# Two graph-attention layers on one core: layer 0's output projection by seven products, its flags and masks, and the order of the last step

## The chip, the cores and the metric

The kernel runs on one core of a Trainium2 chip. The metric is the device time of one execution in microseconds (us). The engines are named as in the profile: PE (matrix multiplication) with PEld (its weight loads), DVE (vector), ACT (scalar and activations), POOL (GpSimd), SP (the queue that issues DMAs).

## The reference

64 graphs of 256 nodes with 512 features each go through two layers. Both normalise, apply a ReLU, attend under an adjacency mask and add the result to their input:

```
# layer 0: 4 heads of 64, inner width 256
h = relu(layernorm(x));  q, k, v = h@Wq, h@Wk, h@Wv
a = softmax(where(adj, q k^T / 8, -max));  x = x + (a v) @ Wo + bo
# layer 1: 8 heads of 64, inner width 512
h = relu(layernorm(x));  q, k, v = split((layernorm(h)*gamma + beta) @ w_qkv^T)
a = softmax(where(adj | eye, q k^T / 8, -1e9));  x = x + (a v) @ w_out^T + b_out
```

In layer 0 a row of the mask without any neighbour gives equal weights; "flags" below (the tile `ne`) say which rows have a neighbour. All inputs but the mask are float32.

## The kernel before

**Steps and order.** A step handles two graphs, 512 tokens; there are 32 (NSTEP). Four tiles of 128 tokens (NT) make the rows `t` = 0 to 3; tiles 0 and 1 are the first graph. The order of instructions on PE, DVE, ACT and POOL is the order in which the program issues them. It comes from a list of events: `at(period, place, fn)` gives a function the key period × PERIOD + place, and at the end all events run in the order of their keys. Layer 0 of a step, layer 1 of the step before and the loads of the step after are so woven together; each engine then works its queue in order, and semaphores hold it where a tile is not ready. SP's DMAs keep the same order.

**Seven products.** The projections of queries and keys (`project_qk`, L755), layer 1's values (`project_v1`, L796) and layer 1's output projection (`combine1`, L821) are each made of seven half-size products instead of eight. `PRODUCT` (L398) names, for each product, the block of the weights and the block of the activations. Sums of blocks are made ahead: of weights once (`weight_sum`, L405), of activations in each step (`act_sums0`, L408, and `act_sums1`, L411 to L413) on POOL. `at_set` (L979) puts the seven one after another in the order `SET` or `SETC`; each has its matmuls at the front of its share and its evacuation from PSUM at the end of it. Products pass through four PSUM banks. `bank_of` (L729) lets product 2 go into the bank of product 1, 4 into that of 7 and 3 into that of 5 (`SHARED`), after the first of each pair has been read out; those banks are held meanwhile. `evacuate` (L684) writes a projection's blocks; `accumulate` (L703) adds a combination's products to the residual `xt` and keeps a common term `u`, which POOL adds to three blocks at L723 (in the last step DVE does).

**Layer 0's output projection** (`combine0`, L807) is plain: for each row tile t two matmuls of 128x128 by 128x512 and one addition to `xt` on DVE (L811). Its four tiles begin at place AT_C0 + 0.01, woven with the transposes of the next step's rows (`transpose_h`, L651, evacuated by ACT at L655 for layer 0 and L661 or L657 for layer 1). The attention outputs stand in `oT0`, one block for each pair of heads.

**Behind it** comes layer 1's normalisation: `norm1` takes the moments of a row of `xt` (L569 and L570 on DVE) and writes the centred ReLU on ACT (L623, L624); `norm1_rest` takes the moments of that, and POOL makes the factors (L639, L640, then `row_scales`, L579 to L581); `scale_row` (L585, ACT) scales the rows, which are then transposed. `norm0`, the same for layer 0, uses L569, L570 and L602.

**Attention of one pair of heads** is spread by `visit` (L986). At one place stand, for the pair before: weighing the values (L896) with ACT's copy to oT (L914), key sums (L930), and on DVE the reciprocals (L940) with their guard (L941), which SP spreads over partitions with eight DMAs (L955) and POOL multiplies in (`normalise`, L960). For the present pair: scores (L853), the masks' addition on DVE (L877), exponentials on ACT (L882) and sums of key halves on POOL (L887). In layer 0 POOL also multiplies two query blocks by the flags (L765).

**Masks.** `masks` (L550) makes both layers' additive masks from the turned adjacency `adT`: n1 first (L555, three buffers), n0 from n1 times the flags (L558), then n1 without its diagonal (L564).

**The ends.** In step 0 weights are still turned into place (`weight_block`, L463 on PE, L468 on DVE and ACT) between the sets. In the last step the order of layer 1 is first query/key set, layer 1's combination of the step before, second query/key set, values; the plain combination of layer 0 stands ahead of the first set.

Of the kernel before, what the change touches and what calls it, by code (L numbers as in the profile page):

```python
# [315 lines left out]
def fast_path(  # L316
# [80 lines left out]
    B_OF = ((0, 8, 7), (1, 3, 1))  # L397
    PRODUCT = {1: (0, 0), 2: (1, 1), 3: (6, 2), 4: (3, 6), 5: (2, 3), 6: (4, 4), 7: (5, 5)}  # L398
# [8 lines left out]
    def act_sums0(b, eng=nc.gpsimd):  # L407
        eng.tensor_tensor(b[:, 3], b[:, 7], b[:, 0], ALU.subtract)  # L408

    def act_sums1(b, eng=nc.gpsimd):  # L410
        eng.tensor_tensor(b[:, 4], b[:, 2], b[:, 3], ALU.subtract)  # L411
        eng.tensor_tensor(b[:, 5], b[:, 2], b[:, 7], ALU.subtract)
        eng.tensor_tensor(b[:, 6], b[:, 1], b[:, 4], ALU.subtract)  # L413
# [3 lines left out]
    HC, HP1 = NC // 2, PR1 // 2  # L417
    wqk0 = const.tile([P, NB, HC, 2, H0], FP, name="wqk0")
    wv0 = const.tile([P, NC, I0], FP, name="wv0")
    wo0 = const.tile([P, PR0, D], FP, name="wo0")  # L420
# [6 lines left out]
    def first_weights():  # L427
        for i in range(2):
            for k, w in enumerate((wq, wk)):
                nc.sync.dma_start(  # L430
                    wqk0[:, 2 * i:2 * i + 2, :, k, :].rearrange("p j c o -> p (j c) o"),
                    w[:, i * H0:(i + 1) * H0].rearrange("(c p) o -> p c o", p=P),
                )
        nc.sync.dma_start(wv0, wv.rearrange("(c p) o -> p c o", p=P))
        nc.sync.dma_start(wo0, wo.rearrange("(c p) o -> p c o", p=P))
        for v, t in ((bo, bo_b), (b_out, bout_b)):
            nc.sync.dma_start(t, bass.AP(tensor=v.tensor, offset=v.offset, ap=[[0, P], [1, D]]))
        gbr = sm.tile([2 * NC, P], FP, name="gbr", tag="inv", bufs=1)
        nc.scalar.dma_start(gbr[:NC], gamma.rearrange("(c p) -> c p", p=P))
        nc.scalar.dma_start(gbr[NC:], beta.rearrange("(c p) -> c p", p=P))  # L440
        return gbr
# [108 lines left out]
    def masks(s):  # L550
        st = S[s]
        adT = st["adT"]
        n1 = st["n1"] = act.tile([P, NIC, G, N], BF, name="n1", bufs=3)
        n0 = st["n0"] = act.tile([P, NIC, G, N], BF, name="n0")
        nc.gpsimd.tensor_scalar(n1, adT, -1.0, BIG, op0=ALU.add, op1=ALU.mult)  # L555

        for kc in range(NIC):
            nc.gpsimd.tensor_tensor(  # L558
                n0[:, kc].rearrange("p g n -> p (g n)"),
                n1[:, kc].rearrange("p g n -> p (g n)"), st["ne"], ALU.mult,  # L560
            )
        for kc in range(NIC):
            v = n1[:, kc, :, kc * P:(kc + 1) * P]
            nc.gpsimd.tensor_tensor(v, v, offdiag, ALU.mult)  # L564
# [7 lines left out]
    def row_scales(s, var, rows=slice(0, NT)):  # L572

        st = S[s]
        if rows.start == 0:
            st["r"] = stat.tile([P, NT], FP, name="r", bufs=3)
            st["mr"] = stat.tile([P, NT], FP, name="mr", bufs=3)
# [37 lines left out]
    def norm1(s, t):  # L615
        st, x1 = S[s], S[s]["xt"]
        if t == 0:
            st["mv"] = stat.tile([P, NT, 3], FP, name="mv1", bufs=2)
            st["mean"] = stat.tile([P, NT, 2], FP, name="mg", bufs=2)
            st["h"] = act.tile([P, NT, D], FP, name="h")  # L620
# [9 lines left out]
    def norm1_rest(s, t):  # L630
        st = S[s]
# [4 lines left out]
        if t % part == part - 1:  # L636
            rows = slice(t + 1 - part, t + 1)
# [3 lines left out]
            row_scales(s, ve, rows)  # L641
# [101 lines left out]
    def project_qk(s, lyr, a, n):  # L743
# [3 lines left out]
        if n == 1:  # L747
            for pr in (a, a + half):
                st["qk", lyr, pr] = sm.tile([P, 2, T], FP, name="qk", bufs=3)
# [53 lines left out]
    def combine0(s, t):  # L803
        st = S[s]
        bank = mm_tile([P, D])
        for pr in range(PR0):
            nc.tensor.matmul(  # L807
                bank, st["oT0"][:, pr, t // NIC, t % NIC * P:(t % NIC + 1) * P], wo0[:, pr, :],
                start=(pr == 0), stop=(pr == PR0 - 1),
            )  # L810
        return lambda: nc.vector.tensor_tensor(st["xt"][:, t, :], bank, st["xt"][:, t, :], ALU.add)  # L811

    def combine1(s, n):
        st = S[s]
        if n == 1:
            st["u"] = sm.tile([P, NIC, HD], FP, name="u", bufs=1)
        bank, first = bank_of(st, "c", n, HD)
        wa, ba = PRODUCT[n]
        for t in range(NIC):
            for c in range(HP1):  # L820
                nc.tensor.matmul(  # L821
                    bank[:, t, :], st["oT1"][:, ba, c, t * P:(t + 1) * P], wo1[:, wa, c, :],
                    start=first and (t, c) == (0, 0), stop=(t, c) == (NIC - 1, HP1 - 1),
                    skip_group_check=True,
                )
        return lambda: accumulate(n, bank, token_rows(st["xt"], HD), st["u"], s == NSTEP - 1)
# [17 lines left out]
    def scores(s, lyr, pr):  # L844
# [21 lines left out]
        if last and pr in (1, 2):  # L866
            pd = (wo0, wv0)[pr - 1].rearrange("p a b -> p (a b)").rearrange("p (e g n) -> p e g n", e=2, g=G)
# [21 lines left out]
    def weigh(s, lyr, pr, first):  # L889
# [11 lines left out]
        if lyr == 0:  # L901
            if first:
                st["oT0"] = act.tile([P, PR0, G, N], FP, name="oT0")
            dst = st["oT0"][:, pr]
        else:
            if first:
                st["oT1"] = act.tile([P, NB + 1, HP1, N], FP, name="oT1")
            b0, b1, step = B_OF[pr // HP1]
            dst = st["oT1"][:, b0:b1:step, pr % HP1, :]
# [56 lines left out]
    PERIOD = 6.13  # L966
# [17 lines left out]
    SETC = (1, 5, 2, 6, 7, 3, 4)  # L984

    def visit(period, w, prev, cur, later=0.0):  # L986

        w -= 0.0003
        if 0 <= prev[0] < NSTEP:
            at(period, w, weigh_out, *prev)  # L990
            at(period, w, key_sums, *prev[:3])
            at(period, w + later, invert, *prev[:3])
            at(period, w + (0.63 if prev[1:3] == (1, 1) else 0.55), normalise, *prev[:3])
        if 0 <= cur[0] < NSTEP:
            at(period, w, scores, *cur)
            at(period, w + later, mask_scores, *cur, 0)
            at(period, w + 0.05, exponentials, *cur, 0)
            at(period, w + 1 / 7, mask_scores, *cur, 1)
            at(period, w + 0.18, exponentials, *cur, 1)
            at(period, w + 0.2, key_halves, *cur, 0)  # L1000
            at(period, w + 0.3, key_halves, *cur, 1)

    AT_C0, AT_Q0, AT_V0, AT_H1, AT_C1 = 3.0, 3.57, 4.57, 5.13, 5.131
    LAST_QK = 4.0
    for s in range(-1, NSTEP - 1):
# [6 lines left out]
        visit(p, 3.685 if tail else AT_Q0 + 2 / 7, (s, 1, 1, False), (s, 1, 3), 0.03 if tail else 0.0)  # L1012
        if s >= 0:
            visit(p, LAST_QK + 3 / 7 if tail else AT_V0, (s, 1, 3, False), (s + 2, 0, 0))
# [3 lines left out]
    for w, i, pr in (  # L1018
        (LAST_QK + 1, 5 / 7, 0), (LAST_QK + 1 + 3 / 7, 5 / 7, 2), (LAST_QK + 3, 5 / 7, 1), (LAST_QK + 3 + 2 / 7, 4 / 7, 3)
    ):  # L1020
        visit(p, w, none, (NSTEP - 1, 1, pr))
        at(p, w + i - 0.0005, key_sums, NSTEP - 1, 1, pr)
        at(p, w + i, invert, NSTEP - 1, 1, pr)
# [8 lines left out]
    for s in range(NSTEP):  # L1032
# [14 lines left out]
        if s < 2:  # L1047
            at(p, (3.72, 2.72)[s], neighbours_rows, s)
            at(p, (3.855, 3.59)[s], neighbours_turn, s)
# [3 lines left out]
        at(p, (3.7125, 3.583)[s] if s < 2 else 2.2, adjacency_turn, s)  # L1053
        at(p, (3.87, 3.74)[s] if s < 2 else 2.75, masks, s)
        if s == 0:
            at(p, AT_C0, first_transposes)
        else:
            for c in range(NC):
                at(p, AT_C0 + 0.14 * (c // 2) + 0.001 * c if s > 1 else 2.9292 + 0.0001 * c, transpose_h, s, 0, c)
        at(p, AT_C0 + 0.1, lambda s=s: act_sums0(S[s]["hT"]))  # L1060
        at(p, AT_C0 + (0.2 if s != 1 else 0.101), lambda s=s: act_sums1(S[s]["hT"]))
# [7 lines left out]
        at(p, 1.0 if s else 0.0, load_x, s)  # L1069
        at(p, 1.8 if s else 1.55, first_bias, s)  # L1070
        back = 0.0 if s else 0.13
        for t in range(NT):
            at_dense(p, AT_C0 + 0.01 + 0.14 * t - back, 0.14, combine0, s, t)
            at(p, AT_C0 + 0.3 + 0.14 * t - back if (s, t) != (NSTEP - 1, 3) else 3.69, norm1, s, t)
            at(p, ((3.55, 3.7, 4.05, 4.2) if s < NSTEP - 1 else (3.55, 3.6, 3.7, 3.705))[t] - back, norm1_rest, s, t)
            at(p, 3.62 + 0.08 * t if 0 < s < NSTEP - 1 else 6.5 + 0.1 * t, second_bias, s, t)
            at(p, 4.5 + 0.1 * t if 0 < s < NSTEP - 1 else (4.25 if s == 0 else 3.71) + 0.003 * t, scale_row, s, t)

        for c in range(NC):
            at(p, (AT_H1 if s < NSTEP - 1 else 3.8) + 0.0001 * c, transpose_h, s, 1, c)  # L1080
        at(p, AT_C1 + 0.15 if s < NSTEP - 1 else 3.95, lambda s=s: act_sums0(S[s]["hT"], nc.gpsimd if s < NSTEP - 1 else nc.vector))
        at(p, AT_C1 + 0.5 if s < NSTEP - 1 else 3.96, lambda s=s: act_sums1(S[s]["hT"], nc.gpsimd if s < NSTEP - 1 else nc.vector))
        p = s
        if s < NSTEP - 1:
# [4 lines left out]
            at(p, 4.55 if not last else LAST_QK + 0.99, lambda s=s: act_sums0(S[s]["oT1"]))  # L1089
            at(p, AT_C1 + 0.1 if not last else LAST_QK + 1.0, lambda s=s: act_sums1(S[s]["oT1"]))  # L1090
            at_set(p, AT_C1 if not last else LAST_QK + 1, SETC, combine1, s)
            at(p, 6.3, store, s)
        else:
            p = s - 1
            at_set(p, LAST_QK, SET, project_qk, s, 1, 0)
            at_set(p, LAST_QK + 2, SET, project_qk, s, 1, 1)
# [3 lines left out]
            at_set(p, LAST_QK + 4.1, (1, 5, 2, 3, 6, 7, 4), combine1, s)  # L1100
# [5 lines left out]
    for i in range(4):  # L1106
        at(-2, 3.01, weight_sum, nc.vector, wqk0, i)
    at(-2, 4.0, lambda: blocks.extend(weight_loads()))
# [63 lines left out]
```

## Time and profile before

| | |
|---|---|
| median of 3 runs (lowest, highest) | 3401.17 us (3400.61, 3402.93) |
| the profiled execution's own time | 3401.54 us |
| its span, first to last instruction | 3399.3 us |
| PE, PEld busy | 3373.3 us (99%), 2621.7 us (77%) |
| DVE, ACT, POOL busy | 1919.5 (56%), 1243.2 (37%), 1991.2 (59%) |
| one step in the middle, by the starts of the same set | 104.69 us |
| first value set of layer 1 begins | 114.2 us |

Each float32 matmul (but for the transposes) stands in the profile as two instructions. A group's row has its line, engine, operation and tiles, the count, the busy time in us and mean ns of one, and then the idle time before them and what ended it. Matmuls overlap, so the mean of one is longer than the distance from start to start. A row of the order of time has start, length in us, engine, line and operation, count, and in brackets an idle time before and who ended it.

### The profile page before, as it was taken

The numbers are of one execution on the slowest core, as the hardware profiler recorded it, in microseconds if no ns is written. First come the engines' busy times: TensorE is split into PE (matmuls) and PEld (weight loads), VectorE is DVE, ScalarE is ACT, GpSimd is POOL, SyncE is SP. The second block draws the span as 40 slices with busy tenths as digits, with TensorE's granted clock in tenths as the row PEclk, the third lists the DMA queues.
The fourth block names the chain that finished last, engine by engine and source line by source line (L and its number), as shares of the span: only waits on it lengthen the run. The fifth ranks groups of instructions, "written<-read, shape, count | busy, mean of one in ns | idle before, by whom it ended". The sixth has DMA issues, their size and how long they took to land.

```text
span 3399.3 us, 59198 instructions
## 1 busy us (share of the span) xinstructions
PE 3373.3 (99%) x22602; PEld 2621.7 (77%) x22602; DVE 1919.5 (56%) x3402; ACT 1243.2 (37%) x2193; POOL 1991.2 (59%) x1858
## 2 busy tenths in 40 slices
PE   8999999999999999999999999999999999999999
PEld 6777777787777877778777777777787777877777
DVE  6755556555565555555555655556555555555565
ACT  4433443333333334433344333343333443334431
POOL 5655665556655556655576556665555655556632
PEclk9999999999999999999999999999999999999999
DMA  4111111211111211111111111111121111111111
GB/s 129 46 56 57 48 39 46 58 57 54 32 48 56 58 54 33 48 55 56 58 43 44 46 58 57 53 32 48 57 58 52 34 47 57 57 58 41 32 41 42
DMA packets 167697, 173.89 MB, mean 51 GB/s; under 512 B 59624, under 2 KB 112368, under 8 KB 167408
## 3 DMA queue, kind: packets, MB, share of 16 engines
q1 hardware_dynamic: 167008, 169.78, 16.9%
q8 instruction: 180, 2.95, 0.4%
q14 instruction: 109, 0.89, 0.1%
q10 hardware_dynamic: 400, 0.27, 0.0%
HBM read 85.99 MB, written 33.62 MB: 35 GB/s over the span
## 4 chain that ended last, share of the span: by engine, by line
PE 97%; DVE 1%; ACT 0%; issue 0%; DMA 0%; POOL 0%; SPq 0%; DVEq 0%; POOLq 0%
PE mm L755 34%; PE mm L796 12%; PE mm L821 11%; PE sc L853 11%; PE sc L896 10%; PE mm L782 6%; PE mm L807 6%; PE mm L651 3%; PE mm L930 2%; PE mm L543 0%; DVE bs L569 0%; ACT h L585 0%; DVE wqk L405 0%; DVE wqkv L405 0%; DVE inv L940 0%
## 5 line engine op out<-in xcount | busy, mean ns | idle before, releaser
L887 POOL TENSOR_TENSOR pd<-p 128x512 f32<-128x512 f32 x378 | 477.2, 1278 | 631.6 <-ACT p L882 523.3
L755 PE MATMUL mm<-hT,wqkv 128*128 128x256 f32 x3584 | 800.0, 382 | 2.6 <-DVE hT L411 1.4
L755 PEld LDWEIGHTS mm<-hT,wqkv 128*128 128x128 f32 x3584 | 673.8, 190 | 112.6 <-issue 23.1
L882 ACT ACTIVATE p<-p 128x512 f32<-128x512 f32 x768 | 459.1, 629 | 478.8 <-DVE p L877 477.9
L940 DVE RECIPROCAL inv<-mm 128x128 f32<-128x128 f32 x384 | 339.7, 926 | 367.6 <-PE mm L930 330.9
L877 DVE TENSOR_TENSOR p<-sc,n 128x512 f32<-128x512 f32 x768 | 481.2, 682 | 4.2 <-PE sc L853 4.2
L914 ACT COPY oT<-sc 128x512 f32<-128x512 f32 x188 | 110.2, 586 | 993.6 <-PE sc L896 993.6
L755 PE MATMUL mm<-hT,wqk 128*128 128x256 f32 x1792 | 403.4, 382 | 0.7 <-ACT wqkv L468 0.6
L796 PE MATMUL mm<-wqkv,hT 128*128 128x256 f32 x1792 | 396.1, 381 | 0.0
L821 PE MATMUL mm<-wo,oT 128*128 128x256 f32 x1792 | 393.3, 379 | 1.0 <-DVE xt L712 0.7
L960 POOL TENSOR_TENSOR oT<-oT,invb 128x512 f32<-128x512 f32 x188 | 240.9, 1282 | 261.0 <-DMA invb<-inv 253.3
L755 PEld LDWEIGHTS mm<-hT,wqk 128*128 128x128 f32 x1792 | 338.4, 191 | 69.5 <-DVE inv L940 9.9
L853 PE MATMUL sc<-qk 64*128 64x256 f32 x3072 | 384.1, 389 | 0.0
L796 PEld LDWEIGHTS mm<-wqkv,hT 128*128 128x128 f32 x1792 | 337.6, 190 | 56.3 <-issue 11.4
L821 PEld LDWEIGHTS mm<-wo,oT 128*128 128x128 f32 x1792 | 337.6, 190 | 47.7 <-issue 1.5
L896 PE MATMUL sc<-p,v 128*32 128x256 f32 x6144 | 370.7, 382 | 0.0
L853 PEld LDWEIGHTS sc<-qk 64*128 64x128 f32 x3072 | 281.2, 186 | 104.2 <-issue 77.6
L896 PEld LDWEIGHTS sc<-p,v 128*32 128x32 f32 x6144 | 180.3, 109 | 162.0 <-issue 61.5
L723 POOL TENSOR_TENSOR xt<-xt,u 128x512 f32<-128x512 f32 x93 | 118.1, 1270 | 245.6 <-DVE xt L716 183.9
L585 ACT ACTIVATE h<-h,mr,r 128x512 f32<-128x512 f32 x252 | 197.4, 809 | 115.4 <-POOL mr L581 115.3
L782 PE MATMUL mm<-wv,hT 128*128 128x256 f32 x1024 | 230.3, 382 | 0.0
L807 PE MATMUL mm<-wo,oT 128*128 128x512 f32 x512 | 230.3, 593 | 0.0
(123 smaller groups left out, 3675.1 us busy)
## 6 DMA issues: line engine op xcount, KB each, us to landing
invb<-inv SPq DMA_DIRECT2D x1528, 32.0 KB, 1.8
xt<-in_x_dram SPq DMA_DIRECT2D x32, 1024.0 KB, 9.8
h<-in_x_dram SPq DMA_DIRECT2D x31, 1024.0 KB, 6.2
out_dram<-xt SPq DMA_DIRECT2D x31, 1024.0 KB, 4.5
ne<-row SPq DMA_DIRECT2D x30, 256.0 KB, 4.4
ad<-in_adj_dram SPq DMA_DIRECT2D x32, 128.0 KB
wr<-in_L_gnn_w_qkv_dram SPq DMA_DIRECT2D x3, 1024.0 KB, 13.5
h<-in_x_dram SPq DMA_DIRECT2D x4, 256.0 KB, 2.7
```

The source lines that it names most:

```text
L755: nc.tensor.matmul(bank[:, k, :], w[:, wa, c, k, a * P:(a + 1) * P], st["hT"][:, ba, c, :], start=first and (k, c) == (0, 0), stop=(k, c) ...
L782: nc.tensor.matmul(bank, st["hT"][:, b0 + t // NIC * step, c % HC, i:i + P], wv0[:, c, :], start=(c == 0), stop=(c == NC - 1),)
L796: nc.tensor.matmul(bank[:, t, :], st["hT"][:, ba, c, t * P:(t + 1) * P], wqkv1[:, wa, c, 2, :], start=first and (t, c) == (0, 0), stop=(t, ...
L807: nc.tensor.matmul(bank, st["oT0"][:, pr, t // NIC, t % NIC * P:(t % NIC + 1) * P], wo0[:, pr, :], start=(pr == 0), stop=(pr == PR0 - 1),)
L821: nc.tensor.matmul(bank[:, t, :], st["oT1"][:, ba, c, t * P:(t + 1) * P], wo1[:, wa, c, :], start=first and (t, c) == (0, 0), stop=(t, c) ...
L853: nc.tensor.matmul(sc[g][e][:, kc, :], qk[rows, 1, k0:k0 + P], qk[rows, 0, g * N:(g + 1) * N], start=True, stop=True,)
L877: nc.vector.tensor_tensor(p[e][:, g], sc[e], neg[:, :, g, :], ALU.add)
L882: nc.scalar.activation(p[e][:, g], p[e][:, g], AF.Exp, scale=SCALE)
L887: eng.tensor_tensor(pd[:, e], p[e][:, :, 0, :], p[e][:, :, 1, :], ALU.add)
L896: nc.tensor.matmul(po[r0:r0 + 32, g, :], st[f"v{lyr}"][:, g * NIC + kc, pr * P + r0:pr * P + r0 + 32], p[r0 // DH][:, g, kc, :], start=(kc ...
L940: nc.vector.reciprocal(inv[:, i * P:(i + 1) * P], sums[:, i * P:(i + 1) * P])
L960: nc.gpsimd.tensor_tensor(dst, dst, invb, ALU.mult)
```

## The change

Layer 0's output projection becomes seven products, by a function that serves both layers. `wo0` and `oT0` get the seven blocks' layout, DVE sums wo0's blocks once and POOL those of oT0 in each step. Both outputs keep seven blocks (`O_OF`) where oT1 had eight. In step 0 and the last step DVE adds the common term, else POOL.

```
-    wo0 = const.tile([P, PR0, D], FP, name="wo0")
+    wo0 = const.tile([P, NB, HP0, HD], FP, name="wo0")
...
-    def combine0(s, t):
-        bank = mm_tile([P, D])
-        for pr in range(PR0):
-            nc.tensor.matmul(
-                bank, st["oT0"][:, pr, t // NIC, t % NIC * P:(t % NIC + 1) * P], wo0[:, pr, :],
-        return lambda: nc.vector.tensor_tensor(st["xt"][:, t, :], bank, st["xt"][:, t, :], ALU.add)
...
+    def combine(s, lyr, n):
         st = S[s]
         if n == 1:
             st["u"] = sm.tile([P, NIC, HD], FP, name="u", bufs=1)
+        oT, w, half = st[f"oT{lyr}"], (wo0, wo1)[lyr], (HP0, HP1)[lyr]
         bank, first = bank_of(st, "c", n, HD)
         wa, ba = PRODUCT[n]
         for t in range(NIC):
+            for c in range(half):
                 nc.tensor.matmul(
+                    bank[:, t, :], oT[:, ba, c, t * P:(t + 1) * P], w[:, wa, c, :],
...
+        at_once = s == NSTEP - 1 or (s, lyr) == (0, 0)
+        return lambda: accumulate(n, bank, token_rows(st["xt"], HD), st["u"], at_once)
...
+    SETC0 = (1, 6, 5, 2, 7, 3, 4)
...
+        at(p, 1.75 if s else 1.8, lambda s=s: act_sums0(S[s]["oT0"]))
+        at(p, 1.76 if s else 2.48, lambda s=s: act_sums1(S[s]["oT0"]))
+        edge = 0 if s == 0 else 1 if s == NSTEP - 1 else 2
+        for i, n in enumerate(SETC0 if s else SETC):
+            if edge == 1:
+                at_dense(p, 1.99905 + 0.00008 * i, 0.00107, combine, s, 0, n)
+            else:
+                at_dense(p, AT_C0 + (-0.12 if s == 0 else 0.14) + i / 14, 1 / 14, combine, s, 0, n)
...
+        at(-2, AT_V0, weight_sum, nc.vector, wo0, i)
```

The masks are made by two functions, each from adT; n1 has two buffers instead of three, the query/key tile two instead of three (the last step's first set uses a free part of wqk0), and in the middle steps n1 is made later, at place 5.7. The flags stay float32.

```
+    def mask0(s):
+        n0 = st["n0"] = act.tile([P, NIC, G, N], BF, name="n0")
+        nc.gpsimd.tensor_scalar(n0, st["adT"], -1.0, BIG, op0=ALU.add, op1=ALU.mult)
         for kc in range(NIC):
+            v = n0[:, kc].rearrange("p g n -> p (g n)")
+            nc.gpsimd.tensor_tensor(v, v, st["ne"], ALU.mult)
+    def mask1(s):
+        n1 = st["n1"] = act.tile([P, NIC, G, N], BF, name="n1", bufs=2)
+        nc.gpsimd.tensor_scalar(n1, st["adT"], -1.0, BIG, op0=ALU.add, op1=ALU.mult)
```

The order changes with it. PERIOD goes from 6.13 to 6.2. The transposes of layer 0 stand together ahead of the combination. The visit that stood after two products of layer 0's query/key set stands before the set, so in the middle of a step the order on PE is transposes, combination, visit, query/key set. The rows of layer 1's norm are taken in the order 2, 3, 0, 1 and later, inside that set:

```
-    AT_C0, AT_Q0, AT_V0, AT_H1, AT_C1 = 3.0, 3.57, 4.57, 5.13, 5.131
-    LAST_QK = 4.0
+    AT_C0, AT_Q0, AT_V0, AT_H1, AT_C1 = 3.0, 3.64, 4.64, 5.2, 5.201
+    LAST_QK = 3.0
...
+    NORM1 = (2, 3, 0, 1)
...
+            at(p, ((3.315, 3.32, 3.39, 3.41), (2.2, 2.25, 2.4, 2.45), (3.79, 3.8, 3.93, 3.94))[edge][k], norm1, s, k)
+                p, ((3.4, 3.42, 3.43, 3.435), (2.3, 2.35, 2.5, 2.55), (4.075, 4.22, 4.23, 4.36))[edge][k],
+                norm1_rest, s, k,
...
+            at(p, 6.5 + 0.1 * k if edge < 2 else AT_V0 + 0.01 * k, second_bias, s, k)
...
-            at_set(p, LAST_QK + 2, SET, project_qk, s, 1, 1)
+            at_set(p, LAST_QK + 1, SET, project_qk, s, 1, 1)
...
-            at_set(p, AT_C1 if not last else LAST_QK + 1, SETC, combine1, s)
+            at_set(p, AT_C1 if not last else LAST_QK + 2, SETC, combine, s, 1)
```

For the last step, layer 0's combination stands right behind layer 1's values of the step before; then come that step's second query/key set, the last step's transposes, its two query/key sets one behind the other, the combination of the step before, and the last values.

## The prediction

> **What bounds the kernel now.** I read the page first (engine shares, then the chain that ended last), then the groups, TensorE's waits, the order of time in one step of the steady middle, and last the two ends with the granted clock.
>
> ```profile
> span 3399.3 us, 59198 instructions
> PE 3373.3 (99%) x22602; PEld 2621.7 (77%) x22602; DVE 1919.5 (56%) x3402; ACT 1243.2 (37%) x2193; POOL 1991.2 (59%) x1858
> ...
> PE 97%; DVE 1%; ACT 0%; issue 0%; DMA 0%; POOL 0%; SPq 0%; DVEq 0%; POOLq 0%
> ```
>
> The chain runs through PE for 97% of the span. In the waits PE stands still from 100 to 3250 us for 0.8 us only; all else lies in the first 100 and the last 150 us. So a matmul left out of a middle step is time saved, if no new wait opens, and a wait of PE's costs its full length.
>
> ```profile
> L821 PE MATMUL mm<-wo,oT 128*128 128x256 f32 x1792 | 393.3, 379 | 1.0 <-DVE xt L712 0.7
> ...
> L807 PE MATMUL mm<-wo,oT 128*128 128x512 f32 x512 | 230.3, 593 | 0.0
> ```
>
> Each matmul of the program stands here as two instructions. L807 is layer 0's combination: 16 instructions a step. L821 is layer 1's, already by seven products: 56 a step. The change turns L807's 16 into 28 of L821's kind. What each takes, in order of time:
>
> ```profile
> 1927.39 1.09 PE L651 MATMUL mm<-ident,h 128*128 128x128 f32 x8
> 1928.32 1.88 PE L807 MATMUL mm<-wo,oT 128*128 128x512 f32 x4
> 1930.04 1.04 PE L651 MATMUL mm<-ident,h 128*128 128x128 f32 x8
> 1930.91 5.32 PE L807 MATMUL mm<-wo,oT 128*128 128x512 f32 x12
> 1936.06 3.62 PE L755 MATMUL mm<-hT,wqk 128*128 128x256 f32 x16
> ...
> 1965.64 12.25 PE L821 MATMUL mm<-wo,oT 128*128 128x256 f32 x56
> 1977.83 1.93 PE L896 MATMUL sc<-p,v 128*32 128x256 f32 x32
> ```
>
> From start to next start L807 takes 1.72 + 5.15 = 6.87 us a step (0.429 each). L821 takes 12.19 for 56, so 6.10 for 28; about 0.09 of the 12.19 is the step into the narrow matmuls of L896, which every such block shows and which exists before and after (without it 0.216 each, 6.05).
>
> **The sum, against the profiled execution's 3401.54 us** (span 3399.3 and 2.2 around it; the median of the three runs is 0.4 lower).
>
> *1. PE work.* Saved per step 6.87 − 6.10 = 0.77 to 6.87 − 6.05 = 0.82, say 0.80: 32 steps, **−25.6**. Nothing else on PE changes in number: the transposes, the block of L896/L930/L853 that moves from inside the first query/key set to before it, and the turns remain.
>
> *2. New waits in the 30 middle steps.* Layer 0's combination had plain sums; now products share banks, and its sums come 3 on POOL and 6 on DVE, with one copy on ACT. Four places are tight. T is the first transpose, S the first score matmul of the next block.
> - Product 4 goes into product 7's bank, and only product 3 (0.86) lies between. Needed: lag to DVE 0.20 (1967.57, where L708 starts, less 1965.64 and a product of 1.73), the add 0.69 (L712), release to PE about 0.15 (the row at 3391.23 starts 0.05 after DVE's end and its first load costs 0.1). 1.04 against 0.86: **0.18** lost. In layer 1 a product is 1.73 and hides this.
> - Product 2 goes into product 1's bank after ACT has copied it. ACT first has four L655 and two exponentials: 0.69 + 4 × 0.49 + 2 × 0.53 + 0.59 = T + 4.3, and PE is there at T + 1.74 + 3 × 0.86 = T + 4.3. I take 0.03; bounds 0 and 0.2.
> - In the query/key set product 4 waits for DVE's evacuation of 7. DVE's queue from S: 0.14, reciprocals and guard 2.15, four masks 2.45, two adds 1.22, and now seven moments pairs ahead, 5.67:
>
> ```profile
> 1935.22 0.69 DVE L569 BATCH_NORM_STATS2 bs<-xt 128x6 f32<-128x512 f32 x1
> 1935.94 0.18 DVE L570 BATCH_NORM_AGGREGATE mv<-bs 128x2 f32<-128x6 f32 x1
> 1936.04 0.66 DVE L569 BATCH_NORM_STATS2 bs<-h 128x6 f32<-128x512 f32 x1
> ...
> 1942.04 1.77 DVE L940 RECIPROCAL inv<-mm 128x128 f32<-128x128 f32 x2 [1.53 <-PE mm L930]
> ```
>
>   (A pair is 0.81 from start to start.) The evacuation starts at S + 11.6, and PE can go on at S + 12.5. PE is there at S + 1.93 + 6 × 1.754 = S + 12.45. **0.05** lost; bounds 0 and 0.4, as everything on DVE in 12 us stands in front of it.
> - POOL's row scales (1.79 from 1950.81 to 1952.60) and then the flag product L765 (1.29) end at about S + 16.25; the scores that need them come at S + 16.5, less 0.15. Hidden by 0.1; if not, up to 0.2.
>
> Together 0.26 a step, **+7.8**; bounds 0.1 and 0.9 a step (3 and 27 us). Each tenth that I miss a step is 3 us.
>
> *3. The head.* Four sums of the new wo0 (128x256, DVE) stand before the last moments of step 1, whose rows PE already awaits (L651). Half of a 128x512 sum: 0.34 (L408 on DVE, 0.68) to 0.85 (L405, up to 1.7 beside POOL); I take 0.45, **+1.8**. Step 0 makes 9 DVE operations instead of 4 (5 × 0.61 = 3.1) in a chain for which PE waits 1.1 us now at L651. ACT's copies of L786 now queue behind the copy of u and the rows of norm1, and hold banks of the next products and weight blocks. I lay out 1.7 at the combination's third product, 0.7 at product 4, 2.7 at the last weight blocks, 0.8 more at the transposes, 1.1 in the first set after. With the sums **+8.8**; bounds 1.4 (the sums alone) and 14.
>
> [...] L405's 128x512 sums took 1.59 us in the mean for wqk, while L411 on DVE took 0.69 alone and 1.57 beside POOL. [...]
>
> *4. The tail.* The last step's combination goes a set forward, behind values instead of behind the second query/key set, so its norm has 15 us more of matmuls beside it. Now:
>
> ```profile
> PE mm L651 <- ACT h L585: 3.0, 4, 1.7
> PE mm L755 <- DVE hT L411: 1.4, 1, 1.4
> ...
> 3302.60:3309.40 6.80, 6.03 (x21) 5.18 (x22) 4.92 (x9) 4.78 (x8) 0.33 (x1) 0.50 0.15 39
> 3309.40:3330.00 20.60, 18.86 (x121) 14.41 (x120) 13.15 (x17) 4.81 (x9) 8.47 (x7) 1.00 0.06 14
> ```
>
> The first two are waits after 3250 us; the last two are stretches, whose third number from the end is PE's granted clock: 0.50 for 6.8 us after the first waits. From the scores at 3297.17 to 3306.68 stand 9.5 us for 3.7 of work (1.94 + 1.80), from there to 3314.96 8.3 for 5.3 (12 × 0.432 and a change): 8.8 lost, 9.8 with the 1.0 at L821. New there: moments and masks of the last step in one query/key set, DVE 2.0 late; the transposes 1.0; the combination's bank and POOL's sums 0.8; the last product's 0.7 remains. 4.5 against 9.8: **−5.3**; bounds −9 (nothing new) and −1.
>
> The rule that speaks against the head here: the clock halved after 3.0 us of waits. [...] If it falls once in the head, where I lay out gaps of 2.2 to 2.6 us, the sum is about 3 us worse.
>
> *Sum:* −25.6 + 7.8 + 8.8 − 5.3 = −14.3 on 3401.54, and 0.4 for the median: **3387 us**. Masks made apart cost POOL 1.05 more a step (the L555 form, 34.0 for 32), second in its queue to nothing PE awaits; POOL has 41% free. If that cover is gone, place four opens.
>
> **The rivals.**
> - *Slower: DVE's queue in the query/key set is the new bound.* 12 us of it are in front of one evacuation with 0.05 to spare on the wrong side. It decides when the four places together reach 0.8 a step: the saving is gone, and the head decides. At 1.0 a step: −25.6 + 30 + 8.8 − 5.3 = +8, 3409. For it: no slack. Against: the row durations are steady (L877 0.68, L940 0.92), and the middle repeats them 30 times.
> - *Eaten:* 0.6 to 0.8 a step; 3397 to 3403, median 3400: no difference.
> - *Hidden:* the waits are 0.1 a step and the head costs 4: −25.6 + 3 + 4 − 6 = −24.6, 3376.
> - *It does not save what it says:* half-width matmuls at more than half the time. The rows refute it (0.216 against 0.429).
>
> **How the numbers follow.** 3387 with its own range 3379 to 3394: 0.60. Hidden: 0.12. Eaten: 0.14. Slower: 0.14. This kernel's three runs lie within 0.07%; I take 0.2% (6.8 us) as what can be told from no change: below 3394.4 faster, above 3408 slower. Eaten lies within 0.2%; of the slower case 0.04 does too, since it decides from 3403 on. Faster 0.72, same 0.18, slower 0.10. The range 3374 to 3403 takes in hidden and eaten and leaves out the slower case and the edge of the hidden one.
>
> **What would show it.** Right: the L821-like group doubles from 1792 to 2688 instructions at 0.216, L807's group is gone; a middle step is 104.15 us, not 104.69; PE waits about 0.2 on DVE's accumulation once a step; no stretch of the tail at clock 0.50; the first value set of layer 1 starts some 8 us later than its 114.2. Wrong: a middle step at 104.5 or more, or PE waits on L765 or the evacuations of a tenth or more each step.

## The result and the profile after

Six runs of the changed kernel have a median of 3389.07 us (3386.89 to 3389.73), six of the kernel before beside them 3402.05 (3400.61 to 3403.35): ratio 0.996, 95% interval 0.995 to 0.9971. The forecast was 3387. The profiled execution took 3387.59 us (before 3401.54).

The page of the changed kernel, the lines that answer to the first ones shown of before:

```profile
span 3385.8 us, 60239 instructions
PE 3354.9 (99%) x22986; PEld 2695.6 (80%) x22986; DVE 1954.2 (58%) x3476; ACT 1232.3 (36%) x2225; POOL 2214.4 (65%) x2108
...
PE 95%; DVE 1%; DMA 0%; SPq 0%; POOL 0%; ACT 0%; issue 0%; POOLq 0%; ACTq 0%
...
L825 PE MATMUL mm<-wo,oT 128*128 128x256 f32 x2688 | 599.4, 381 | 3.1 <-issue 1.5
L825 PEld LDWEIGHTS mm<-wo,oT 128*128 128x128 f32 x2688 | 501.3, 190 | 82.7 <-DVE xt L721 10.7
```

PE still carries the chain, with 18 us less busy time. L825 is now the combination of both layers: 2688 instructions, and the group of 512 wide ones is gone. One middle step in order of time, and then what line L825 waited for between 130 and 3200 us:

```profile
1199.57 1.97 PE L660 MATMUL mm<-ident,h 128*128 128x128 f32 x16
1201.38 6.42 PE L825 MATMUL mm<-wo,oT 128*128 128x256 f32 x28
1207.73 1.94 PE L902 MATMUL sc<-p,v 128*32 128x256 f32 x32
```

```profile
its engine sat idle before it (us, times) until:
  DVE xt L721: 9.6, 30
  ACT u L717: 4.7, 30
```

From start to next start layer 0's combination takes 6.35 us. 28 instructions of 0.216 and the 0.09 into the narrow matmuls make 6.14; 0.21 is waiting, once a step for DVE's additions (L721) and once for ACT's copy of u. (The idle times in the view are those of the weight loads, which run ahead of the matmuls: in this step from 1201.3 to 1207.2 us, the matmuls from 1201.4 to 1207.4. The view has 9.6 and 4.7 us in 30 steps, so 0.32 and 0.16 a step; the matmuls themselves start less late.) Read start by start in the trace (medians over the steps), the first matmul of product 4 begins 0.084 late, the one behind it 0.104 late, and product 2 0.02. A step takes 104.073 us (before 104.686).

The head before, at three marks (the first value tile of step 1, the weighing behind layer 1's first transposes, the first value set of layer 1):

```profile
64.21 1.89 PE L782 MATMUL mm<-wv,hT 128*128 128x256 f32 x8
...
87.83 1.93 PE L896 MATMUL sc<-p,v 128*32 128x256 f32 x32
...
114.20 6.09 PE L796 MATMUL mm<-wqkv,hT 128*128 128x256 f32 x27
```

The changed kernel's head, in order of time and then in stretches (the third number from the end is PE's granted clock):

```profile
65.94 1.89 PE L795 MATMUL mm<-wv,hT 128*128 128x256 f32 x8
...
74.30 4.55 PE L825 MATMUL mm<-wo,oT 128*128 128x256 f32 x20 [1.55 <-issue]
...
87.39 1.97 PE L468 MATMUL mm<-ident,wr 128*128 128x128 f32 x8 [2.63 <-ACT v L799]
...
95.21 1.93 PE L902 MATMUL sc<-p,v 128*32 128x256 f32 x32
...
109.09 6.41 PE L768 MATMUL mm<-hT,wqkv 128*128 128x256 f32 x16 [2.33 <-DVE qk L700]
...
125.27 5.01 PE L809 MATMUL mm<-wqkv,hT 128*128 128x256 f32 x22
```

```profile
83.85:87.26 3.41, 0.91 (x9) 0.67 (x7) 3.27 (x9) 2.03 (x6) 0.19 (x1) 1.00 0.00 0
87.26:90.67 3.41, 3.28 (x14) 2.76 (x16) 1.78 (x6) 2.20 (x9) 2.57 (x8) 0.50 0.00 0
...
104.33:107.74 3.41, 1.43 (x10) 0.87 (x8) 3.41 (x6) 2.06 (x6) 3.41 (x3) 1.00 0.19 48
107.74:111.15 3.41, 2.06 (x5) 1.70 (x6) 2.38 (x4) 1.80 (x5) 3.41 (x4) 0.50 0.12 29
111.15:114.57 3.42, 3.42 (x10) 2.71 (x9) 1.66 (x2) 0.00 (x0) 3.42 (x3) 0.50 0.00 0
```

The first value set of layer 1 begins at 125.27 us, before at 114.20. Two waits of PE each stand in a stretch after which the clock is at half, for 3.41 and for 6.83 us. In the tail, what PE waited for after 3200 us (in total, times, longest):

```profile
PE mm L768 <- DVE qk L704: 1.3, 1, 1.3
PE mm L825 <- DVE xt L721: 0.7, 1, 0.7
PE mm L825 <- POOL oT L412: 0.4, 1, 0.4
PE mm L660 <- ACT h L591: 0.4, 1, 0.4
```

2.8 us instead of 5.4, and the clock stays up through the last matmuls. By spans:

| part | before | after | difference | forecast |
|---|---|---|---|---|
| to the first value set of layer 1 | 114.20 | 125.27 | +11.1 | +8.0 |
| 30 steps | 30 × 104.686 | 30 × 104.073 | −18.4 | −16.2 |
| from step 30's value set to the end | 144.5 | 138.3 | −6.2 | −6.1 |
| span | 3399.3 | 3385.8 | −13.5 | −14.3 |

(The forecast's 0.80 for PE's work stands in each part once for each of its combinations: 8.8 − 0.8, 30 × (0.26 − 0.80), −5.3 − 0.8.)

### The profile page after: what moved, and what is told of

Read it like the earlier page. It is cut to its first block, busy times and chain, and to the rows that moved or that the text cites. A ratio compares the mean times of both kernels' runs of the same rounds, so it can differ in the third digit from the quotient of the medians.

```text
span 3385.8 us, 60239 instructions
## 1 busy us (share of the span) xinstructions
PE 3354.9 (99%) x22986; PEld 2695.6 (80%) x22986; DVE 1954.2 (58%) x3476; ACT 1232.3 (36%) x2225; POOL 2214.4 (65%) x2108
## 4 chain that ended last, share of the span: by engine, by line
PE 95%; DVE 1%; DMA 0%; SPq 0%; POOL 0%; ACT 0%; issue 0%; POOLq 0%; ACTq 0%
PE mm L768 33%; PE mm L825 17%; PE mm L809 11%; PE sc L859 11%; PE sc L902 10%; PE mm L795 6%; PE mm L660 3%; PE mm L935 2%; PE mm L548 0%; SPq L960 0%; DVE inv L945 0%; DMA xt<-in_x_dram 0%; DMA out_dram<-xt 0%; DVE p L883 0%; DVE bs L575 0%
## 5 line engine op out<-in xcount | busy, mean ns | idle before, releaser
L768 PE MATMUL mm<-hT,wqkv 128*128 128x256 f32 x3584 | 801.9, 383 | 3.8 <-DVE qk L700 2.3
L768 PEld LDWEIGHTS mm<-hT,wqkv 128*128 128x128 f32 x3584 | 676.2, 191 | 113.6 <-issue 21.6
L825 PE MATMUL mm<-wo,oT 128*128 128x256 f32 x2688 | 599.4, 381 | 3.1 <-issue 1.5
L825 PEld LDWEIGHTS mm<-wo,oT 128*128 128x128 f32 x2688 | 501.3, 190 | 82.7 <-DVE xt L721 10.7
L768 PE MATMUL mm<-hT,wqk 128*128 128x256 f32 x1792 | 398.5, 383 | 0.7 <-ACT wqkv L473 0.6
L809 PE MATMUL mm<-wqkv,hT 128*128 128x256 f32 x1792 | 395.5, 382 | 0.0
L768 PEld LDWEIGHTS mm<-hT,wqk 128*128 128x128 f32 x1792 | 337.6, 191 | 57.6 <-issue 10.3
L809 PEld LDWEIGHTS mm<-wqkv,hT 128*128 128x128 f32 x1792 | 338.6, 190 | 54.5 <-issue 10.7
L902 PE MATMUL sc<-p,v 128*32 128x256 f32 x6144 | 370.7, 382 | 0.0
L732 POOL TENSOR_TENSOR xt<-xt,u 128x512 f32<-128x512 f32 x183 | 230.7, 1276 | 165.3 <-DVE xt L725 150.6
L902 PEld LDWEIGHTS sc<-p,v 128*32 128x32 f32 x6144 | 180.7, 110 | 160.9 <-issue 61.7
L721 DVE TENSOR_TENSOR xt<-mm,xt 128x512 f32<-128x512 f32 x128 | 88.2, 689 | 328.1 <-PE mm L825 328.0
L795 PE MATMUL mm<-wv,hT 128*128 128x256 f32 x1024 | 230.4, 383 | 0.1
```

The lines of the kernel that those rows point to most:

```text
L732: (nc.vector if last else nc.gpsimd).tensor_tensor(r, r, u, ALU.add)
L768: nc.tensor.matmul(bank[:, k, :], w[:, wa, c, k, a * P:(a + 1) * P], st["hT"][:, ba, c, :], start=first and (k, c) == (0, 0), stop=(k, c) ...
L795: nc.tensor.matmul(bank, st["hT"][:, b0 + t // NIC * step, c % HC, i:i + P], wv0[:, c, :], start=(c == 0), stop=(c == NC - 1),)
L809: nc.tensor.matmul(bank[:, t, :], st["hT"][:, ba, c, t * P:(t + 1) * P], wqkv1[:, wa, c, 2, :], start=first and (t, c) == (0, 0), stop=(t, ...
L825: nc.tensor.matmul(bank[:, t, :], oT[:, ba, c, t * P:(t + 1) * P], w[:, wa, c, :], start=first and (t, c) == (0, 0), stop=(t, c) == (NIC - ...
L902: nc.tensor.matmul(po[r0:r0 + 32, g, :], st[f"v{lyr}"][:, g * NIC + kc, pr * P + r0:pr * P + r0 + 32], p[r0 // DH][:, g, kc, :], start=(kc ...
```

## The experiments

Each edit is on the changed kernel.

**1 and 2. Is the 0.2 us of a step the wait for product 7's bank?** One order puts another product between 7 and 4, the other puts 4 right behind 7. (The last step has the same order.)

```
-    SETC0 = (1, 6, 5, 2, 7, 3, 4)
+    SETC0 = (1, 6, 5, 7, 2, 3, 4)      # one run
+    SETC0 = (1, 5, 6, 2, 3, 7, 4)      # the other
```

> Layer 0's products in the middle steps in the order 1, 6, 5, 7, 2, 3, 4: two products now stand between product 7 and product 4, which adds into 7's bank, and three between 1 and 2. Theory (the wait for product 7's bank): the first matmul of product 4 lost 0.084 us and the start after it 0.104 us in the changed kernel's trace, product 2 lost 0.02; all three go. A step takes 103.86 to 103.90 us instead of 104.07, and the time is 3383 to 3384 us, 5 to 6 under the changed kernel's 3389.1. Rival (the 0.2 us belong to any set of products that is entered or left, whatever its order): a step stays at 104.07 and the time at 3389.

> The same products in the order 1, 5, 6, 2, 3, 7, 4: product 4 right behind product 7, no product between them. Theory (the wait for product 7's bank): 4 waits for one product's length more, 0.86 us (four starts of 0.216), so a step takes 104.93 us, of which 30 make 26 us: 3415 us, slower than the kernel before. Rival (no bank wait): 104.07 and 3389.

Measured: 3382.83 us with a step of 103.862, and 3415.36 with a step of 104.940. The middle of the first, then of the second:

```profile
1201.02 6.21 PE L825 MATMUL mm<-wo,oT 128*128 128x256 f32 x28
1207.16 1.93 PE L902 MATMUL sc<-p,v 128*32 128x256 f32 x32
```

```profile
1212.26 5.37 PE L825 MATMUL mm<-wo,oT 128*128 128x256 f32 x24
1218.41 1.13 PE L825 MATMUL mm<-wo,oT 128*128 128x256 f32 x4 [0.78 <-DVE xt L721]
1219.48 1.93 PE L902 MATMUL sc<-p,v 128*32 128x256 f32 x32
```

6.14 us without a wait, and 7.22 with the wait in plain sight ahead of product 4's four instructions. Each product between the two is worth its own length (0.87 a step from 4 behind 7 to one between) until the wait is used up (0.21 for the next). In the second order the bank's whole hold stands open: in the median of the steps product 4's first matmul starts 0.95 late and the next another 0.10, together 1.05 where the prediction had 1.04. The bank is shown; the rival is out.

**3. How far was the "slower" rival?** One more instruction on DVE in each middle step:

```
         moments(mg, h, t)
+        if 0 < s < NSTEP - 1 and k in (0,):
+            nc.vector.bn_stats(stat.tile([P, 6], FP, name="bx"), h[:, t, :])
```

> In each of the 30 middle steps DVE takes the moments of one row once more (one instruction of 0.60 us from start to start, its result unused), ahead of the query/key set's evacuation of product 7. In the changed kernel's trace that evacuation ends 0.25 us before PE starts product 4 in the same bank, and where PE does wait for DVE it starts 0.1 to 0.2 after DVE's end: a margin of 0.05 to 0.15. Theory (nearly no margin, as the rival 'slower' of the prediction has it): 0.45 to 0.6 a step, a step of 104.55 to 104.7 us, and 3403 to 3407 us, the whole gain of the change. Rival (DVE has air there, 58% busy): 104.07 and 3389.

Measured: 3404.84 us, ratio 1.0008 (0.9998 to 1.0017) to the kernel before, a step of 104.633, 0.56 more. In the query/key set product 4 now waits for DVE's evacuation of 7:

```profile
1218.13 10.63 PE L770 MATMUL mm<-hT,wqk 128*128 128x256 f32 x48
1229.08 1.97 PE L770 MATMUL mm<-hT,wqk 128*128 128x256 f32 x8 [0.32 <-DVE qk L706]
```

The added instruction moved that evacuation by 0.59 (medians of the middle steps, counted from the set's start). Product 4's first matmul starts 0.48 late and the next another 0.08, together the 0.56 of the step; so the margin was 0.59 − 0.48 = 0.11 us. The changed kernel's trace says the same: from the evacuation's end to product 4 it is 0.25, and where PE waits for it, 0.15. DVE is busy 58% of the span, and one instruction of it at this place takes the whole gain.

**4. The tail.** The last step goes back to the old order: `LAST_QK` = 4.0, four plain tiles ahead of the first query/key set, and the old places of their norm and scores.

```
-    LAST_QK = 3.0
+    LAST_QK = 4.0
...
+            at_dense(p, AT_C0 + 0.01 + 0.14 * k, 0.14, combine_plain, s, k)
...
-                at_dense(p, 1.99905 + 0.00008 * i, 0.00107, combine, s, 0, n)
...
-            at_set(p, LAST_QK + 1, SET, project_qk, s, 1, 1)
+            at_set(p, LAST_QK + 2, SET, project_qk, s, 1, 1)
```

> The last step goes back to its old order: layer 0's combination by four plain token tiles ahead of the first query/key set, then the combination of layer 1, then the second set; the middle is as changed (one block of wo0 is restored by one subtraction on DVE before it). Theory (a set of matmuls beside the last norm hides what PE waited for): from the value set of step 30 to the end 138.3 us become 143.5 to 145, the waits for the rows of the last norm and the half clock near the end come back, and the time is 3394 to 3396 us. Rival (the tail got shorter by the products and the masks alone): 138 to 140, and 3389 to 3391.

Measured: 3395.57 us; 144.5 us from step 30's value set to the end, and after 3200 us the old waits:

```profile
PE mm L660 <- ACT h L591: 3.7, 2, 3.4
PE mm L768 <- DVE hT L412: 2.7, 1, 2.7
PE mm L825 <- DVE xt L721: 0.7, 1, 0.7
```

The half clock is back too (3.41 us). The edit also gives back the 0.8 us of PE work that the seven products save in the last step, so of the 6.2 us some 5.4 are the order's: 7.1 us of waits for 2.8, and the half clock. Most of the tail's gain is the set of matmuls beside the last norm.

**5. The head.** Six runs take it apart. Its end alone misleads, since in seven of the twelve experiments the clock also fell at some 21 us, after a wait of 2.1 to 2.4 us at L535 (1.79 in the changed kernel, without a fall), which made all that follows some 1.7 to 2.0 us later (with plain tiles in step 0, for one, the forty L768 behind it took 10.56 us for 8.87). So I read three marks: the first value tile of step 1 (L795), the weighing behind layer 1's first transposes (L902), and the first value set (L809).

| kernel | first tile | to the weighing | to the value set | value set | median, us |
|---|---|---|---|---|---|
| before | 64.21 | 23.62 | 26.37 | 114.20 | 3402.05 |
| changed | 65.94 | 29.27 | 30.06 | 125.27 | 3389.07 |
| plain tiles in step 0 | 65.61 | 26.49 | 29.09 | 121.19 | 3383.49 |
| PE kept busy in two gaps | 67.73 | 29.69 | 28.19 | 125.61 | 3386.49 |
| weight blocks back | 66.05 | 29.27 | 26.21 | 121.53 | 3383.78 |
| weight blocks and value tiles back | 67.74 | 28.38 | 26.23 | 122.35 | 3384.49 |

Plain tiles in step 0 (`combine_plain`: for each tile eight half-width matmul instructions and one addition). The places of step 0's layer-1 norm, which follows the tiles, are moved with them and are not shown:

```
+        for k in range(NT if s == 0 else 0):
+            at_dense(p, AT_C0 + 0.01 + 0.14 * k - 0.13, 0.14, combine_plain, s, k)
-        for i, n in enumerate(SETC0 if s else SETC):
+        for i, n in enumerate(SETC0 if s else ()):
...
-        at(-2, AT_V0, weight_sum, nc.vector, wo0, i)
+        at(0, 1.5 + 0.1 * i, weight_sum, nc.vector, wo0, i)
```

> Step 0 alone combines layer 0 as before the change: four token tiles, one addition each, with half-width matmuls on the unsummed weight blocks; the sums of wo0 are made in step 0's middle, and its sums of oT0 are left out. Theory (the head's 11 us come from the products of step 0: their ten additions on DVE for four, the waits behind them, and the half clock that these waits bring): the first value set of layer 1 begins at 114 to 116 us instead of 125.3, the clock does not fall in the head or falls once, and the time is 3378 to 3381 us. By the terms of the prediction alone (1.8 + 1.7 + 0.7 - 0.8, and some 3 for the clock) it would be 3382 to 3386. Rival (the head is longer because the sets and weight blocks were moved to other places): it begins at 122 to 125 us and the time stays within 3 us of 3389.

Measured 3383.49 us, within the terms of the prediction and not as low as my theory: the stretch to the weighing is only 2.8 us shorter, and the clock fell at 21 and at 106 us (the sixteen L768 at 106.01 took 5.41 us; in the next run, at full clock, 3.72). (The ten additions of the theory are, in the changed kernel's trace, nine on DVE and the copy of u on ACT.)

Unused matmuls in the gaps:

```
+    def filler(n):
+        sc = ps_sc.tile([P, NIC, N], FP, name="sc")
+        for _ in range(n):
+            nc.tensor.matmul(sc[:, 0, :], ident, wv0[:, 0, :N], start=True, stop=True)
...
+    at(-1, 1.77, filler, 5)
+    at(0, 0.2, filler, 6)
```

> The changed kernel with unused matmuls on PE in two gaps of the head: 10 matmul instructions of 0.216 us ahead of the weight transposes that waited until 87.39 us, 12 ahead of those at 106.11. Nothing reads their result. Theory (the clock was halved twice in the head, each time after a stretch of 3.41 us in which PE had been busy for 0.91 and 1.43 us, and the halves lie on the path): the clock stays at 1.00 there and the first value set begins 2 to 5 us earlier than 125.27; the time is 3384 to 3387 us. Rival 1 (the halves fall in time in which PE waits anyway): the clock stays up and the value set begins at 125 all the same. Rival 2 (the clock falls for another cause): the two halves stay.

```profile
86.39 2.32 PE L853 MATMUL sc<-wv,ident 128*128 128x256 f32 x10
...
94.51 0.33 PE L660 MATMUL mm<-ident,h 128*128 128x128 f32 x1 [2.31 <-ACT h L591]
...
97.42 3.13 PE L907 MATMUL sc<-p,v 128*32 128x256 f32 x32
...
112.12 3.72 PE L768 MATMUL mm<-hT,wqkv 128*128 128x256 f32 x16 [1.04 <-DVE qk L700]
```

Both theory and rival 1 are half right. The sixteen L768 take 3.72 us where they took 6.41 at half clock: the second fall had cost 2.7. The first had cost nothing: from the first tile to the first L660 it is 26.78 us in both kernels, since PE, faster now, waits 2.31 for ACT's scaled rows instead of 0.77. The stretch from 93.07 to 96.48, in which most of that wait lies, has 1.60 us of matmuls; behind it the clock was at half, and the weighing took 3.13 for 1.93. Here the filled gap moved the idle time: 2.63 us ahead of the weight blocks became 0.47, and 0.77 ahead of the transposes 2.31.

Weight blocks back:

```
-        place = ... else 6.2 + 1 / 7 * (i - 12)
+        place = ... else 6.27 + 1 / 7 * (i - 12)
```

> The last four weight blocks of the head are issued 0.07 later (6.27 for 6.2), so that product 5 of the first set comes before the third of them again, as it did while the unit of the places was 6.13. Nothing else is changed. Theory (this order, by itself, holds the product behind a block whose bank and copy are late, and the PE gap that it makes halves the clock for two stretches): from the first weight block between the products to the value set the head is 1.1 to 1.5 us shorter by the order and up to 2.7 more if the clock stays up; the first value set begins at 121 to 124.2 us instead of 125.27, and the time is 3385 to 3388. Rival (the products and the wait for DVE's first evacuation set the time there, in either order): 125 and 3389.

```profile
106.40 1.99 PE L768 MATMUL mm<-hT,wqkv 128*128 128x256 f32 x8 [1.19 <-ACT wo L473]
109.21 0.66 PE L468 MATMUL mm<-ident,wr 128*128 128x128 f32 x4 [0.82 <-DVE qk L700]
...
121.53 10.84 PE L809 MATMUL mm<-wqkv,hT 128*128 128x256 f32 x49
```

3383.78 us, with the value set where the theory had it. The edit only undoes a side effect: these four blocks stand at a place counted from the end of a period, so the change of PERIOD from 6.13 to 6.2 had put them 0.07 earlier and the third of them ahead of product 5. With 5 first again PE waits 1.19 and 0.82 where it waited 1.00 and 2.33, the clock stays up, and the stretch to the value set loses 3.85 us: 2.7 of clock and some 1.2 of order. It is then as long as before the change (26.21 for 26.37).

Value tiles back as well (`-0.33 if t < 2 else 0.22` for `-0.26 ... 0.29`, their old distance from the weight blocks):

> The changed kernel with two places of the head set back to where they stood relative to the rest before the unit of the places grew by 0.07: the last four weight blocks (as in the run that moved them alone, first value set at 121.53 us), and now also step 1's value tiles of layer 0 (-0.33 and 0.22 for -0.26 and 0.29), so that the second tile's copy on ACT comes ahead of two weight blocks again. Theory (the head's wait of 1.55 us in the middle of the products comes from the order of ACT's copies, which the unit changed): that wait goes, at most 0.9 of it comes back as a wait of the value tile itself, and the first value set begins at 119.8 to 121 us; 3382 to 3383.5 us. Rival (DVE's ten additions and the norm's chain set the head in any order of the copies): 121.5 and 3383.8.

The stretch to the weighing is 0.9 us shorter, as expected. The time does not show it: 3384.49 us, nearer to the rival's number. In the profiled execution the first tile came 1.7 us late after the early fall of the clock; whether the other three runs had that fall too is not known.

**6. What helps, together.** First the products in the order 1, 6, 5, 7, 2, 3, 4, plain tiles in step 0, weight blocks back, and the value tiles' copies earlier on ACT:

> All that helped, together: the middle's products in the order 1, 6, 5, 7, 2, 3, 4; step 0 with four plain token tiles and the sums of wo0 after it; the last four weight blocks 0.07 later; and in the head ACT's copies of layer 0's values ahead of the copies of the weight blocks and of the second half of the norm. Theory (the parts add up): a step of 103.86 us (-6), the first value set at 111.5 to 115 us instead of 125.3 (-10 to -14), the tail as changed: 3369 to 3374 us. Rival (the head's parts cover one another, since the norm's chain on DVE and ACT sets the head whatever PE does): the value set at 118 to 121, and 3376 to 3380 us.

3376.58 us, in the rival's range, and the value set at 121.83, later than even the rival had it. PE's own work had been pulled ahead of the norm, so it waited 3.63 us in one piece at the transposes, and the clock fell for 6.83 us. The same with unused matmuls in three gaps, and beside it the same order and fillers with products kept in step 0:

> The kernel that joins all helpful parts (3376.6 us; its first value set at 121.83, with the clock halved at 21 us for 3.41 us, at 89 us for 6.83 and at 106 us for 3.41) with unused matmuls at three places of PE's queue where it waited: 8 instructions of 0.216 us ahead of the flag matmuls at 19.90, 10 ahead of the scores at 84.57, 6 ahead of product 5 at 106.22. Theory (in that kernel the halves lay on the path: 1.7 at the first place, 2.5 at the transposes and weighed values, 1.6 at product 5): the clock stays at 1.00 in the head, the first value set begins at 115.5 to 117.5 us, and the time is 3370 to 3373 us. Rival (a filled gap only moves the idle time, and the clock falls at the next gap): one or two halves stay, 119 to 122, and 3374 to 3377.

> The changed kernel with products in step 0 as well, the middle's products in the order 1, 6, 5, 7, 2, 3, 4, the last four weight blocks 0.07 later, and unused matmuls at four places where PE waits in the head (8 instructions at 19.90, 10 ahead of the third pair of weight blocks, 6 ahead of the scores, 6 ahead of product 5). Theory (products in step 0 cost the head 4 to 6 us whatever the clock does: the sums of wo0, ten additions on DVE for four, and the copies behind them): the first value set begins at 119.5 to 122 us, 4 to 6 later than in the kernel with plain tiles in step 0, and the time is 3375 to 3379. Rival (the plain tiles' gain was the clock's): within 2 us of that kernel.

3373.85 us with one fall left (119.15), as the rival had it, and 3377.87 with none (121.70; 29.28 to the weighing, 26.23 to the value set). The second time is in its theory's range, but its value set is 2.6 us behind the first kernel's and not 4 to 6. With the clock up throughout, the head with products is what it was with the weight blocks back alone: the clock at 87 us does not hold it. Last, the value tiles and the first norm's places back where they were:

> The best kernel so far (plain tiles in step 0, the middle's order 1, 6, 5, 7, 2, 3, 4, weight blocks back, unused matmuls in three gaps; 3373.9 us, first value set at 119.15 with the clock halved once) with step 1's value tiles and the first norm's places back where the kernel before had them, and 6 instead of 10 unused instructions ahead of the scores. Theory: PE waits 1 to 2 us less between the value tiles and the transposes, and the first value set begins at 115 to 118 us, 3370 to 3373. Rival (the norm's chain sets it as before): 119 and 3374.

```profile
span 3368.8 us, 60270 instructions
...
82.66 1.46 PE L867 MATMUL sc<-wv,ident 128*128 128x256 f32 x6
...
88.62 1.93 PE L921 MATMUL sc<-p,v 128*32 128x256 f32 x32
...
114.88 11.49 PE L809 MATMUL mm<-wqkv,hT 128*128 128x256 f32 x52
```

3370.92 us, as the theory had it, ratio 0.9909 (0.9893 to 0.9926) to the kernel before, the best of all: 24.33 us to the weighing, 26.26 to the value set, no fall of the clock. Against the run with weight blocks and value tiles back the stretch to the weighing is 4.05 shorter, with six unused instructions in it: that is the price there of step 0's products and of the norm's order that comes with them. The two were changed together and are not told apart.

## Why the prediction was right

1. *PE work.* Forecast 0.80 a step; the order without a wait has 104.686 − 103.862 = 0.82. Right.
2. *Waits of the middle.* Forecast 0.26: 0.18 for product 7's bank, 0.03 for u, 0.05 in the query/key set, nothing for POOL's flag product. Measured 0.084 + 0.104, 0.02, 0 and 0, together 0.21, and the first two orders show the bank to be the cause. The third place, the query/key set, has a margin of 0.11 where I had a wait of 0.05. Over 30 steps steps 1 and 2 gave 2.2 us more than forecast.
3. *Head.* Forecast +8.0, measured +11.1. The sums of wo0: 1.8 forecast, 65.94 − 64.21 = 1.73 (POOL stood idle beside them, from 32.4 to 36.1 us). To the weighing: 1.7 + 0.7 + 2.7 + 0.8 − 0.8 = 5.1 forecast, 29.27 − 23.62 = 5.65 measured: 0.9 for the order of ACT's copies, 4.05 for the products and the norm's order with the other orders back (2.8 in the run with plain tiles alone), and 0.7 not taken apart. Wait by wait the trace has 1.55 for the 1.7 (at the second product, not the third), 0.48 for the 0.7 and 2.63 for the 2.7. At the transposes PE waited 1.1, as before, where I had 0.8 more; it came there later, since the weight blocks and scores just ahead of them took some 1.5 us longer at half clock. The set behind: 1.1 forecast, 3.69 measured. This term was mis-sized, by the 2.7 us that the half clock put on the sixteen L768; the 1.1 by itself is near what the order of the weight blocks costs (some 1.2), but the prediction does not name that order: here its number is luck. The prediction named a fall of the clock, at "about 3 us worse" (half of the 6.8 us at clock 0.50 in the tail before would be 3.4), and left it out of the sum. It had gaps of 2.2 to 2.6 us in mind, and the clock fell at both waits of about that size: at the weight blocks ahead of the transposes (2.63, at 87.39), where the fall cost nothing up to the transposes, and at the 2.33 ahead of the sixteen L768.
4. *Tail.* Forecast −6.1 with the saved PE work, measured −6.2; the old order, which gives up the saved work as well, gives all of it back. The parts fit less well than the sum: of the 4.5 us laid out as lost in the new tail, PE's waits are 2.8. What makes up the rest was not taken apart.

The misses of the head (+3.1) and of the middle (−2.2) nearly cancel, so the total is closer than its terms; that is luck. Of the rivals, "slower" was the near one, at one DVE instruction's distance. "Hidden" and "eaten" would have needed steps of 104.0 and 104.5 or more.

## What to carry to other kernels

Where partial products share PSUM banks, the order of the products is worth checking against the time that the evacuation takes: product 7 one place earlier was worth 6 us here, and right ahead of the product that waits for its bank it cost 26. A unit of a schedule that is changed for the middle also moves everything that is placed from its end; look at the order of the ends afterwards. Look at the clock behind a wait of PE as well as at the wait: here one of 2.33 us was followed by sixteen matmul instructions that took 6.41 us at half clock and 3.72 at full.

## What the runs showed of the hardware

*What stood ahead of a half clock.* Stretches of about 3.41 us with the matmuls in them, and the granted clock in what came next:

| kernel | stretch, us | matmuls in it, us | clock behind it |
|---|---|---|---|
| before | 3299.17 to 3302.59 | 1.17 | 0.50 for 6.83 us |
| changed | 83.85 to 87.26 | 0.91 | 0.50 for 3.41 us |
| changed | 104.33 to 107.74 | 1.43 | 0.50 for 6.83 us |
| PE kept busy in two gaps | 93.07 to 96.48 | 1.60 | 0.50 for 3.41 us |
| changed | 3377.71 to 3381.12, last matmuls | 1.57 | 1.00 for 3.41 us |
| changed | 90.67 to 94.09 | 2.28 | 1.00 |
| changed | 70.19 to 73.61 | 2.56 | 1.00 |

In none of the four that a fall followed did PE stand still throughout; the wait that ended at 87.39 was 2.63 us long. At L535 in the head the clock fell behind waits of 2.08 to 2.43 us (seven experiments) and not behind 1.49 to 1.89 (before, changed, weight blocks back, one more DVE instruction). Where the limit lies, or whether there is a sharp one, these runs do not show: 1.60 us of matmuls stood ahead of a fall, 1.57 did not. At half clock, stretches with 2.63 us of matmuls (before, 3302.59 to 3306.00) and 2.06 (changed, 107.74 to 111.15) were followed by half clock again, those with 3.41 (before, 3306.00 to 3309.41), 3.28 and 3.42 (changed, to 90.67 and to 114.57) by the full one.

*What came behind a wait of PE.* Where the first matmul of product 4 waited 0.084 us in the changed kernel, the next began 0.104 late, in the median of the steps; with no wait, in the first order, both were on time. Behind the wait of 0.95 in the second order it was 0.104 as well, behind the 0.48 of the run with one more DVE instruction 0.075, and behind the 0.02 of product 2 nothing. The forecast had 0.10 for the first load after a wait; that held for a wait of 0.084, shorter than itself, but not for the shortest.
